# Earlier conditions, a reordered gate and shorter seams in a fused mixture-of-experts, attention and feed-forward kernel

## The chip, the cores and the metric

The kernel runs on one core of a Trainium2 chip. The metric is the device time of one execution in microseconds (us), lower is better. In the text PE is TensorE (matrix engine), DVE is VectorE, ACT is ScalarE, POOL is GpSimd and SP is SyncE, which here only issues transfers. "PEld" is the loading of weights into PE.

## The reference

Everything is float32. The input x has 4 sequences of 512 tokens with 256 features; there is also one condition vector of 64 values per sequence.

```
x   = x + linear_attention(mixture_of_experts(x, condition))
out = x + two_local_layers(condition_attention(x, condition))

mixture_of_experts: gate = rmsnorm(x) @ wg + wg_b + condition @ gg_W + gg_b       # 8 experts
                    the two largest of softmax(gate), each times
                    relu(relu(x W1 + b1) W2 + b2) W3 + b3 of its expert
linear_attention:   blocks of 32 tokens, 8 heads, features elu(q proj) + 1, elu(k proj) + 1
                    out = num * 1 / (qp . sum(kp) + 1e-8), then @ w_out.T + b_out
condition_attention: 16 heads over 512 tokens, the weights scaled by
                    sigmoid(tanh([x, condition] Wc1 + bc1) Wc2 + bc2), renormalised;
                    0.79 of that plus 0.21 of a field weight fa:
                    fp = layernorm(relu(condition We1 + be1) We2 + be2),
                    fa = softmax(fp @ sin-table.T)
two_local_layers:   token shift, local attention with window 128, GEGLU feed-forward, twice
```

What the change calls "the conditions" is the part that needs the condition vector alone: condition @ Wc1 (`csb`), the vector `fp`, and the field weights `fa`, transposed to `faT`. They depend on no token, and are used only in the condition attention.

## The kernel before

**Stages.** One program goes through the stages in time: gate and routing (0 to 40 us of the span), expert slots (40 to 321), a conditional block for two rare slots and the weighted sum of the experts' results (321 to 337), linear attention (337 to 500), condition attention (500 to 745), the two local layers (745 to 1427). A scheduler orders each engine's instructions. Inside a region `with PE.in_order()` PE's order is the order in which the code is written; generators are advanced by `next` to weave two pieces of work into each other.

**Gate.** The tokens are loaded into `xres[0..3]`, each 128 partitions x 1024. PE first multiplies the condition with the gate's weights (`pgb`), then transposes the tokens (`pxt`, 32 transposes). The copies `xT` from the accumulators alternate between ACT and DVE (`evac`). ACT squares a batch at once (line 1167), DVE sums it (`ss`, line 1168). PE computes the logits (`pg`); a Sqrt and a reciprocal give `rstd`; `pgt` transposes the logits back and DVE forms `gate` (lines 1192 and 1195). A long DVE chain then picks the two experts and gives every chosen token a row (`rowtok`, line 1342).

**Expert slots.** 20 slots always run, two more (`NRARE`) run under `tc.If`. A slot has 128 or 256 token rows of one expert. `loads` brings that expert's weights with three SP transfers whose address depends on the routing. `gather` fetches the token rows with POOL's indirect transfers and transposes them (`pxb`, `xbT`). `layer` makes h1 and h2 (`ph`, then a relu on ACT or DVE in turn), and `last` makes `po`, adds the bias and scatters the rows to `ys` in DRAM. The first gather is covered by filler matmuls, `busy(4)`; `busy(n)` is n products of the identity with `xres[0]`, whose results nobody reads. They appear as `pbusy`.

**Loads and conditions.** The table `later` holds 15 loads of weights of the next stages (among them `rows`, the 795 KB of row constants `crows`), one is issued per slot from slot 2 on. `conditions` runs ahead of the last of the 20 slots: `pcs` (condition times weights), `pfp`, a DVE and ACT chain to `fp` (lines 241 to 251), `pfpT` (its transpose), `pfs` (512 field logits), an Exp to `fa` (line 263), `pfaT`.

**Seam of the conditional block.** After it come `busy(13)` and four batches of: two loads `g` of 512 KB each (line 1477, from `ys`), four ACT products (line 1481), four DVE sums to `ymoe` (line 1482).

**Linear attention.** `front(b)` adds the constant row `bo` to `xres[b]` on POOL (line 1496), transposes `ymoe` to `yT` and makes `qk` (`pqk`) and `v`. `features` gives `pf` and `f`, `scores` gives `sc`, `values` gives `pn`, `pz`, the reciprocal `z` (line 1565) and `aT` (line 1566), `tail` gives `pao` and adds it into `xres[b]` (line 1576). The accumulators of the features come from the pool `fe`. After the last `tail`, the condition attention begins with its own `front(0)`: transposes `pt` of `xres[0]`, `xT2`, then `pcq`, `pck`, `pcv` and the coherence products `pct`, before the first attention scores (`sc`, `cex`).

Of the kernel before, what the change touches and what calls it, by code (L numbers as in the profile page):

```python
# [63 lines left out]
def adaln_attn_ffn_kernel(ctx: ExitStack, tc: tile.TileContext, a: dict, out: bass.AP):  # L64
# [141 lines left out]
    def cond_weights(pool, queued=lambda name, load: load()):  # L206
        loads = {
            "rows": lambda: load_rows("crows", pool),
            "wqkv": lambda: weight("cwqkv", [128, 2, 3 * H], chunks(a["c_wqkvT"]), pool),
            "hmask": lambda: weight("hmask", [128, 10], a["hmask"], pool),  # L210
            "wout": lambda: weight("cwout", [128, 2, H], chunks(a["c_woT"]), pool),
# [16 lines left out]
    def conditions(W, cp):  # L228
# [22 lines left out]
        nc.vector.tensor_tensor(fp, fp, row("lnb")[:B, :], ALU.add)  # L251
        pt = tpt("pfpT")
# [12 lines left out]
        nc.vector.tensor_scalar(fa, fa, fsum, FIELD, ALU.mult, ALU.mult)  # L265
        pt = tpt("pfaT")
# [6 lines left out]
    def cond_stage(W, cp, sp, safe):  # L273
        csb, faT = W["csb"], W["faT"]
        y = [resp.tile([128, NT, H], F32, tag="res", name=f"yc{b}") for b in range(B)]
        if not safe:

            v1s = []
            for i in range(2):
                v1 = cp.tile([128, NT, CH, 32], F32, tag=f"v1{i}", name=f"v1{i}", bufs=1)  # L280
                nc.gpsimd.memset(v1, 0.0)
                nc.gpsimd.memset(v1[:, :, :, CHD : CHD + 1], 1.0)
                v1s.append(v1)

        def front(b, d):
            xT2 = cp.tile([128, 2, S], F32, tag="xT2", name="xT2")
            xs = cp.tile([128, 2], F32, tag="xs", name="xs")
            for c in range(2):
# [3 lines left out]
                nc.vector.tensor_copy(xT2[:, c, :], pt)  # L292
# [8 lines left out]
            kT = cp.tile([128, 2, S], F32, tag="kT", name="kT")  # L301
            for c in range(2):
# [6 lines left out]
                yield  # L309
                ps = mmt("pck")  # L310
                mm(ps, [(W["wqkv"][:, k, H + c * 128 : H + (c + 1) * 128], xT2[:, k, :]) for k in range(2)])
                nc.vector.tensor_scalar(kT[:, c, :], ps, col("bk", c), None, ALU.add)
# [211 lines left out]
        run(front(0, ds[0]))  # L524
# [23 lines left out]
    def local_stream(dw, lp, y, dr):  # L548
# [264 lines left out]
        ds = [SimpleNamespace(ps={}, oT={}) for b in range(B)]  # L813
        with PE.in_order():
            run(front(wa, 0, ds[0]))
# [292 lines left out]
    with ExitStack() as abc:  # L1108
# [7 lines left out]
        with ExitStack() as moe:  # L1116
# [27 lines left out]

            wgs = xp.tile([128, 2, 32], F32, tag="wgs", name="wgs")
# [6 lines left out]
            with PE.in_order():  # L1152
                pgb = acct("pgb")
                for b in range(B):
                    PE.matmul(pgb[:, b * NE : (b + 1) * NE], csB[:, b, :], ggw, start=True, stop=True)
                xTs = []
                for b in range(B):
                    if b % 2 == 0:
                        xT = ew.tile([128, 4, ME], F32, tag="w2", name="xT")
                    for c in range(2):  # L1160
# [3 lines left out]
                        evac(xT[:, b % 2 * 2 + c, :], pt)  # L1164
# [276 lines left out]
            for j, d in enumerate(often):  # L1441
                if j == len(often) - 1:
                    conditions(cw_, wp)
# [42 lines left out]
        with ExitStack() as lin:  # L1486
# [65 lines left out]
            def values(d, g):  # L1552
                if g == 0:
                    d.aT = lp.tile([128, 2, S], F32, tag="aT", name="aT")
# [217 lines left out]
```

## Time and profile before

| what | value |
|---|---|
| median of three runs | 1429.75 us (1427.66 to 1430.11) |
| the profiled execution's own time | 1429.31 us |
| its span | 1427.5 us (1.8 us of the time lie around it) |
| instructions | 19422 |
| mean granted TensorE clock | 0.981 |
| PE busy 0 to 40 / 40 to 321 / 321 to 337 | 19.6 of 40.0 / 275.1 of 281.0 / 12.9 of 16.0 us |
| PE busy 337 to 500 / 500 to 745 / 745 to 1427 | 143.9 of 163.0 / 236.7 of 245.0 / 666.0 of 682.0 us |
| granted clock in those stages | 0.79, 1.00, 0.89, 0.94, 0.99, 0.99 |

How to read the views: a row of the timeline has the start, the busy time, the engine, the line, the operation, its output and inputs, the shape, and how many instructions it joins; in brackets stands the idle time before it on its engine and what ended it. Most matmuls have the line of one helper (L78 a product, L82 a transpose), so they are told apart by the name of their output. One float32 product has two records. In the table of waits the columns are the total, how often, and the longest. The granted clock is the share of full speed that PE was given; at 0.5 a matmul takes twice as long.

### The profile page before, as it was taken

Reading aid. Unit: us, or ns where it says so; the run is one execution under the profiler, and the core shown is the slowest. Engines: PE = TensorE matmul, PEld = TensorE weight load, DVE = VectorE, ACT = ScalarE, POOL = GpSimd, SP = SyncE. Lnnn points to the kernel's source line nnn. Section 1 sums busy time; section 2 is a strip of 40 time slices with the busy share of each in tenths; the row PEclk is TensorE's granted clock in tenths of the full one; section 3 lists DMA queues with packets and bytes.
Section 4 is the critical chain, followed back from the end, with each engine's and each line's share of the span. In section 5 each row is a group of like instructions: output and inputs, shape, how many; then the busy total and the mean of one; then the engine's idle time right before and its main releaser. Section 6 shows DMA issues by size and latency. Waiting matters only on the chain.

```text
span 1427.5 us, 19422 instructions
## 1 busy us (share of the span) xinstructions
PE 1354.0 (95%) x7624; PEld 835.6 (59%) x7624; DVE 667.0 (47%) x1297; ACT 586.0 (41%) x969; POOL 230.4 (16%) x219
## 2 busy tenths in 40 slices
PE   4999999998899799999999999999999999999998
PEld 3788888874566543333335555656655456556564
DVE  6222221223677642333226777754352767854331
ACT  3111111123555325554654647563222567474111
POOL 0324232111000020000102322100020312310010
PEclk8999999999999899999999999999999999999999
DMA  3577667623000000000111011211001010011000
GB/s 122 216 258 264 223 227 247 214 79 122 1 2 1 0 1 0 1 1 1 44 49 64 2 36 35 75 33 30 22 0 41 23 32 23 17 39 47 14 23 25
DMA packets 43645, 94.74 MB, mean 66 GB/s; under 512 B 9760, under 2 KB 25752, under 8 KB 40728
## 3 DMA queue, kind: packets, MB, share of 16 engines
q1 hardware_dynamic: 38984, 83.11, 17.6%
q0 software_dynamic: 3552, 9.70, 2.0%
q8 instruction: 63, 1.03, 0.3%
q10 hardware_dynamic: 1008, 0.58, 0.2%
q14 instruction: 38, 0.31, 0.1%
HBM read 84.08 MB, written 7.21 MB: 64 GB/s over the span
## 4 chain that ended last, share of the span: by engine, by line
PE 66%; DVE 5%; ACT 3%; issue 2%; DMA 1%; SPq 0%; DVEq 0%; POOL 0%; POOLq 0%
PE pdq L78 11%; PE pug L78 5%; PE sc L78 5%; PE pua L78 5%; PE pv L78 5%; PE pn L78 4%; PE pfy L78 4%; PE pdy L78 4%; PE pds L78 4%; PE pz L78 2%; PE pqt L82 2%; PE pqk L78 2%; PE pcq L78 1%; PE pur L78 1%; PE pcv L78 1%
## 5 line engine op out<-in xcount | busy, mean ns | idle before, releaser
L78 PE MATMUL pdq<-wqkv,yT 128*128 128x512 f32 x384 | 177.6, 603 | 4.5 <-ACT yT L583 4.5
L403 ACT ACTIVATE cex<-sc 128x1024 f32<-128x1024 f32 x128 | 124.1, 1021 | 95.8 <-PE sc L78 94.7
L78 PE MATMUL ph<-h,w 128*128 128x256 f32 (+1 forms) x704 | 133.4, 347 | 1.0 <-ACT h L1356 0.5
L653 DVE TENSOR_TENSOR p<-p,lmask 128x384 f32<-128x384 f32 (+1 forms) x128 | 98.4, 786 | 66.5 <-ACT p L651 65.0
L609 POOL TENSOR_TENSOR qr<-t,t 128x512 f32<-128x512 f32 x64 | 85.8, 1340 | 247.5 <-DVE t L606 229.8
L78 PEld LDWEIGHTS ph<-h,w 128*128 128x128 f32 x704 | 116.2, 191 | 13.3 <-DVE h L1358 0.7
L78 PEld LDWEIGHTS pdq<-wqkv,yT 128*128 128x128 f32 x384 | 69.5, 190 | 82.2 <-issue 72.8
L1358 DVE TENSOR_SCALAR h<-ph,w 128x256 f32<-128x256 f32 (+1 forms) x88 | 36.1, 438 | 164.5 <-PE ph L78 101.5
L1356 ACT ACTIVATE h<-ph,w 128x256 f32<-128x256 f32 (+1 forms) x88 | 35.4, 438 | 187.1 <-PE ph L78 132.5
L651 ACT ACTIVATE p<-pds,ss 128x256 f32<-128x256 f32 (+1 forms) x256 | 95.6, 457 | 35.8 <-PE pds L78 27.3
L78 PE MATMUL pug<-hT,w 128*128 128x512 f32 x160 | 78.3, 612 | 0.0
L599 ACT ACTIVATE sq<-pdq 128x512 f32<-128x512 f32 x64 | 38.3, 598 | 96.7 <-PE pdq L78 57.6
L78 PE MATMUL sc<-qm,kT 32*128 32x512 f32 x512 | 76.0, 647 | 0.0
L78 PE MATMUL pua<-hT,w 128*128 128x512 f32 x160 | 75.6, 595 | 0.0
L78 PE MATMUL pv<-cex,v 128*32 128x512 f32 x512 | 69.0, 604 | 1.7 <-DVE xT L292 1.7
L78 PE MATMUL ph<-xbT,w 128*128 128x256 f32 (+1 forms) x352 | 68.3, 346 | 0.0
L78 PE MATMUL po<-w,h 128*128 128x256 f32 x296 | 67.7, 380 | 0.5 <-ACT h L1356 0.5
L78 PE MATMUL pdy<-wo,oT 128*128 128x256 f32 x256 | 63.3, 392 | 3.3 <-DVE oT L693 3.3
L78 PE MATMUL pds<-qT,kT 64*128 64x256 f32 (+1 forms) x512 | 65.3, 375 | 0.0
L78 PEld LDWEIGHTS pds<-qT,kT 64*128 64x128 f32 x512 | 43.9, 186 | 32.9 <-issue 26.2
L78 PEld LDWEIGHTS ph<-xbT,w 128*128 128x128 f32 x352 | 58.4, 191 | 6.9 <-issue 0.9
L78 PE MATMUL pfy<-w,uA 128*128 128x256 f32 x256 | 61.2, 382 | 0.0
(294 smaller groups left out, 2103.5 us busy)
## 6 DMA issues: line engine op xcount, KB each, us to landing
w<-in_moe_w_dram SPq DMA_DIRECT2D x22, 1024.0 KB
w<-in_moe_w_dram SPq DMA_DIRECT2D x22, 640.0 KB
w<-in_moe_w_dram SPq DMA_DIRECT2D x22, 516.0 KB
zb<-rows SPq DMA_DIRECT2D x32, 256.0 KB
g<-ys SPq DMA_DIRECT2D x8, 512.0 KB
wqkv<-in_f_wqkv_dram SPq DMA_DIRECT2D x2, 1536.0 KB
w<-in_f_w_dram SPq DMA_DIRECT2D x2, 1408.0 KB
xres<-in_x_dram SPq DMA_DIRECT2D x4, 512.0 KB
```

The costliest lines, as they stand in the source:

```text
L78: cls._queue(nc.tensor.matmul(*args, **kw))
L82: cls._queue(nc.tensor.transpose(*args, **kw))
L403: nc.scalar.activation(ex, pss[j], AF.Exp, scale=CHD**-0.5)
L599: nc.scalar.activation(sq, p3, AF.Square)
L609: nc.gpsimd.tensor_tensor(qr_t[:, s], t1, t2, ALU.add)
L651: nc.scalar.activation(p[:, at], pss[r][:, at], AF.Exp, scale=d.ss[:, 2 * u + jj, 1, 2 * c + r : 2 * c + r + 1])
L653: nc.vector.tensor_tensor(p[:, :n], p[:, :n], lmask[:, :n], ALU.mult)
L1356: nc.scalar.activation(dst, src, AF.Relu, bias=bias)
L1358: nc.vector.tensor_scalar(dst, src, bias, 0.0, ALU.add, ALU.max)
```

## The change

- Gate: `pgb` comes after the transposes; all eight `xT` copies go to DVE; each batch is squared by four ACT instructions that also sum (`accum_out`), and the DVE sums go away. The reciprocal of `rstd` keeps its place in the program order.
- Conditions: their weights and `rows` are loaded right behind the tokens. `conditions` becomes a generator with three pieces: the first ahead of `busy(4)`, the second after the products of slot 0, the third after those of slot 1. The table `later` shrinks to nine loads.
- The instruction order after the change also puts the POOL additions of `bo` for batches 1 to 3 ahead of the first gather; they need only the tokens and `rows` and the readers of the tokens to be done.
- Seam of the conditional block: `busy(3)` stands before it and `busy(6)` after it. `results(b)` issues the loads of batch b, in halves for batch 0; those of batches 2 and 3 are issued in `front(0)` and `front(1)`. `weighted(0)` stays at the seam, `weighted(1..3)` move into `front(b)`.
- Seam to the condition attention: the last `tail` is handed to `cond_stage` and woven into `front(0)`, in which `pck` now precedes `pcq`; for batch 0 ACT makes `xT2` and `kT`. The last batch's `aT` and `awo` move to the pool `wp`, the last reciprocal and product are split in halves, the two PSUM pools of the stage change places, and the tiles `v1` are set later.
- Seam to the local layers: the first `front` is taken out of the pinned region.

```diff
@@ cond_weights / conditions
+            "wout": lambda: weight("cwout", [128, 2, H], chunks(a["c_woT"]), pool),
             "wqkv": lambda: weight("cwqkv", [128, 2, 3 * H], chunks(a["c_wqkvT"]), pool),
             "hmask": lambda: weight("hmask", [128, 10], a["hmask"], pool),
-            "wout": lambda: weight("cwout", [128, 2, H], chunks(a["c_woT"]), pool),
...
         nc.vector.tensor_tensor(fp, fp, row("lnb")[:B, :], ALU.add)
+        yield
         pt = tpt("pfpT")
...
         nc.vector.tensor_scalar(fa, fa, fsum, FIELD, ALU.mult, ALU.mult)
+        yield
         pt = tpt("pfaT")
@@ cond_stage
-    def cond_stage(W, cp, sp, safe):
+    def cond_stage(W, cp, sp, safe, before=()):
...
-                nc.vector.tensor_copy(xT2[:, c, :], pt)
+                (nc.scalar.copy if b == 0 else nc.vector.tensor_copy)(xT2[:, c, :], pt)
...
+            if not safe and b < 2:
+                make_v1()
+            for c in range(2):
+                ps = mmt("pck")
+                mm(ps, [(W["wqkv"][:, k, H + c * 128 : H + (c + 1) * 128], xT2[:, k, :]) for k in range(2)])
+                if b == 0:
+                    nc.scalar.activation(kT[:, c, :], ps, AF.Identity, bias=col("bk", c))
+                else:
+                    nc.vector.tensor_scalar(kT[:, c, :], ps, col("bk", c), None, ALU.add)
+                yield
...
-                ps = mmt("pck")
-                mm(ps, [(W["wqkv"][:, k, H + c * 128 : H + (c + 1) * 128], xT2[:, k, :]) for k in range(2)])
-                nc.vector.tensor_scalar(kT[:, c, :], ps, col("bk", c), None, ALU.add)
-                yield
...
-        run(front(0, ds[0]))
+        first = front(0, ds[0])
+        with PE.in_order():
+            for _ in range(4):
+                next(first)
+            for _ in before:
+                next(first)
+        run(first)
@@ local layers
+        run(front(wa, 0, ds[0]))
         with PE.in_order():
-            run(front(wa, 0, ds[0]))
@@ gate
+            cw_ = {}
+            soon = ("rows", "wc1c", "we1", "we2", "peT", "csT")
+            loads_ = cond_weights(wp, lambda name, load: load)
+            for name in soon:
+                cw_[name] = loads_.pop(name)()
...
-                pgb = acct("pgb")
-                for b in range(B):
-                    PE.matmul(pgb[:, b * NE : (b + 1) * NE], csB[:, b, :], ggw, start=True, stop=True)
...
-                        evac(xT[:, b % 2 * 2 + c, :], pt)
+                        nc.vector.tensor_copy(xT[:, b % 2 * 2 + c, :], pt)
...
-                    nc.scalar.activation(sq, xres[b], AF.Square)
-                    nc.vector.reduce_sum(ss[:, b * NT : (b + 1) * NT], sq, axis=AX.X)
+                    for t in range(NT):
+                        nc.scalar.activation(sq[:, t, :], xres[b][:, t, :], AF.Square,
+                                             accum_out=ss[:, b * NT + t : b * NT + t + 1])
+                pgb = acct("pgb")
+                for b in range(B):
+                    PE.matmul(pgb[:, b * NE : (b + 1) * NE], csB[:, b, :], ggw, start=True, stop=True)
...
-            nc.vector.reciprocal(rstd, rstd)
+            tc.keep_in_program_order(nc.vector.reciprocal(rstd, rstd))
@@ expert slots
+            aside = conditions(cw_, wp)
+            next(aside)
             busy(4)
...
-                "awo": lambda: weight("awo", [128, 2, H], chunks(a["a_woT"]), wl),
+                "awo": lambda: weight("awo", [128, 2, H], chunks(a["a_woT"]), wp),
...
+                **loads_,
             }
-            cond_weights(wp, lambda name, load: later.update({name: load}))
...
-                if j == len(often) - 1:
-                    conditions(cw_, wp)
...
                 d.h2 = layer(d, h1, "h2", d.w2, 4)
+                next(aside, None)
             last(len(often) - 1, often[-1])
+
+            busy(3)
             with tc.If(halves > NHALF - NRARE):
...
-            busy(13)
-            for b in range(B):
-                gs = []
-                for k in range(2):
-                    g = gp.tile([128, NT, H], F32, tag=f"g{k}", name=f"g{k}", bufs=2)
-                    at = 1 + (k * B + b) * S
-                    nc.sync.dma_start(g, ys[at : at + S].rearrange("(t p) h -> p t h", p=128))
-                    gs.append(g)
+            busy(6)
+            def results(b):
+                gs = [gp.tile([128, NT, H], F32, tag=f"g{k}", name=f"g{k}", bufs=2) for k in range(2)]
+                n = 2 if b == 0 else NT
+                for t in range(0, NT, n):
+                    for k in range(2):
+                        at = 1 + (k * B + b) * S + t * 128
+                        nc.sync.dma_start(gs[k][:, t : t + n, :],
+                                          ys[at : at + n * 128].rearrange("(t p) h -> p t h", p=128))
+                return gs
+
+            def weighted(b, gs):
                 for t in range(NT):
                     i = b * NT + t
                     nc.scalar.mul(gs[0][:, t, :], gs[0][:, t, :], tops[0][:, i : i + 1])
                     nc.vector.scalar_tensor_tensor(
                         y[b][:, t, :], gs[1][:, t, :], tops[1][:, i : i + 1], gs[0][:, t, :], ALU.mult, ALU.add)
+            both = {b: results(b) for b in range(2)}
+            weighted(0, both[0])
@@ linear attention
             def front(b, d):
+                if b:
+                    weighted(b, both[b])
+                if b + 2 < B:
+                    both[b + 2] = results(b + 2)
...
-                    d.aT = lp.tile([128, 2, S], F32, tag="aT", name="aT")
+                    pool, tag = (wp, "aTlast") if d is ds[-1] else (lp, "aT")
+                    d.aT = pool.tile([128, 2, S], F32, tag=tag, name="aT")
...
-                nc.vector.reciprocal(z, z)
-                nc.vector.tensor_tensor(d.aT[:, g, :], pn, z, ALU.mult)
+                n = S // 2 if d is ds[-1] and g == 1 else S
+                for at in range(0, S, n):
+                    half = slice(at, at + n)
+                    nc.vector.reciprocal(z[:, half], z[:, half])
+                    nc.vector.tensor_tensor(d.aT[:, g, half], pn[:, half], z[:, half], ALU.mult)
...
-            run(tail(B - 1, ds[B - 1]))
+            end = tail(B - 1, ds[B - 1])
...
+            sp = cst.enter_context(tc.tile_pool(name="sp", bufs=3, space=PSUM, reuse_waits="tile"))
             cst.enter_context(banks("ps1", mm=2))
-            sp = cst.enter_context(tc.tile_pool(name="sp", bufs=3, space=PSUM, reuse_waits="tile"))
...
-            y = cond_stage(cw_, cp, sp, False)
+            y = cond_stage(cw_, cp, sp, False, end)
```

More of the change, by code (lines that the diff above doesn't have):

```diff
@@ L271, in conditions, with make_v1 @@
         W["csb"], W["faT"] = csb, faT
-    def cond_stage(W, cp, sp, safe):
+    def cond_stage(W, cp, sp, safe, before=()):
         csb, faT = W["csb"], W["faT"]
         y = [resp.tile([128, NT, H], F32, tag="res", name=f"yc{b}") for b in range(B)]
[L276 to L283, printed above, removed]
+        v1s = []
+        def make_v1():
+            i = len(v1s)
+            v1 = cp.tile([128, NT, CH, 32], F32, tag=f"v1{i}", name=f"v1{i}", bufs=1)
+            nc.gpsimd.memset(v1, 0.0)
+            nc.gpsimd.memset(v1[:, :, :, CHD : CHD + 1], 1.0)
+            v1s.append(v1)
         def front(b, d):
@@ L1429, in adaln_attn_ffn_kernel @@
                 "aqkv": lambda: weight("awqkv", [128, 2, 3 * H], chunks(a["a_wqkvT"]), wl),
-                "awo": lambda: weight("awo", [128, 2, H], chunks(a["a_woT"]), wl),
+                "awo": lambda: weight("awo", [128, 2, H], chunks(a["a_woT"]), wp),
                 "aproj": lambda: weight("aproj", [128, 2, 2, NF], a["a_proj"], wl),
                 "bmask": lambda: weight("bmask", [128, 4, 128], a["bmask"], wl),
+                **loads_,
             }
-            cond_weights(wp, lambda name, load: later.update({name: load}))
-            cw_ = {}
             ds = [SimpleNamespace() for _ in SLOTS]
@@ L1642, in adaln_attn_ffn_kernel @@
                 W = cond_weights(wp)
-                conditions(W, wp)
+                run(conditions(W, wp))
                 y = cond_stage(W, cp, None, True)
```

## The prediction

> **What bounds the kernel now.** I read the page first, then TensorE's waits, then the windows and the timeline at the places the change touches. All times in us unless said.
>
> ```profile
> PE 1354.0 (95%) x7624; PEld 835.6 (59%) x7624; DVE 667.0 (47%) x1297; ACT 586.0 (41%) x969; POOL 230.4 (16%) x219
> ```
>
> TensorE (PE) is busy 95% of the 1427.5 span and is 66% of the chain that ended last. Anything that does not close a PE hole, shorten PE work in PE's own order, or end a half-clock stretch is worth nothing. The waits that PE has at the seams in question:
>
> ```profile
> PE pgb L78 <- DVE csB L1150: 7.8, 1, 7.8
> ...
> PE pao L78 <- DVE aT L1566: 5.0, 2, 3.9
> ...
> PE pbusy L78 <- issue: 3.4, 1, 3.4
> PE pqk L78 <- DVE yT L125: 3.3, 3, 2.1
> ...
> PE pfpT L82 <- DVE fp L251: 1.5, 1, 1.5
> ```
>
> The columns are total, times, longest. In the timeline the conditions cost PE time in the last slots (own work plus a wait for `fp`), and the If seam is thirteen filler passes and what follows:
>
> ```profile
> 308.79 0.28 PE L82 MATMUL pfpT<-ident,fp 4*128 4x4 f32 x2 [1.46 <-DVE fp L251]
> 309.33 1.88 PE L78 MATMUL pfs<-peT,fpT 128*4 128x512 f32 x4 [0.26 <-DVE fpT L256]
> ```
> ```profile
> 324.11 13.09 PE L78 MATMUL pbusy<-xres,ident 128*128 128x512 f32 x26 [3.38 <-issue]
> 324.44 10.76 SPq L1477 DMA_DIRECT2D g<-ys  x8
> ...
> 329.79 1.67 DVE L1482 SCALAR_TENSOR_TENSOR ymoe<-g,m,g 128x256 f32<-128x256 f32 x4 [8.59 <-DMA g<-ys]
> ...
> 337.04 1.04 PE L82 MATMUL pt<-ident,ymoe 128*128 128x128 f32 x8
> ...
> 337.16 3.77 DVE L1482 SCALAR_TENSOR_TENSOR ymoe<-g,m,g 128x256 f32<-128x256 f32 x4 [2.91 <-ACT g L1481]
> 337.29 2.57 POOL L1496 TENSOR_TENSOR xres<-xres,crows 128x1024 f32<-128x1024 f32 x1 [13.20 <-PE pbusy L78]
> ...
> 340.85 0.68 DVE L125 COPY yT<-pt 128x512 f32<-128x512 f32 x1
> ...
> 341.58 4.54 PE L78 MATMUL pqk<-yT,awqkv 128*128 128x512 f32 x6 [2.10 <-DVE yT L125]
> ```
>
> Three things: the first batch's sum is ready at 331.5, but its transposes sit behind the filler until 337.04; then four DVE sums take 3.77 where the same four took 1.67, while POOL adds `bo`; and `yT` queues behind them. The last seam is the wait for the reciprocal and its slow aftermath:
>
> ```profile
> 490.19 3.35 DVE L1565 RECIPROCAL z<-z 128x512 f32<-128x512 f32 x1 [2.75 <-ACT z L1564]
> ...
> 494.40 5.31 PE L78 MATMUL pao<-awo,aT 128*128 128x256 f32 x12 [3.90 <-DVE aT L1566]
> ```
>
> [...] after the hole of 490 to 494 the granted clock is 0.50 from 494 to 498. [...]
>
> **The change, part by part** (minus is a gain; starts and durations are of the profiled execution, 1429.31, whose span is 1427.5; the median is 1429.75, 0.44 above it. 0.2%, about 2.9, is what a measurement can tell from no change).
>
> 1. *Gate.* PE does its 32 transposes before the four `pgb` pairs; DVE takes all eight `xT` copies (0.64 each); four ACT squares (1.06) and four DVE reductions (1.2) become 16 ACT squares that sum themselves. Price: 0.43 for a 128x256 ACT (1.71/4 at L1481) plus 0.18 for the accumulator read at L263: 16 x 0.61 = 9.8 from 5.53 gives 15.3; table load 1.28, `rstd` 0.31, reciprocal 0.25: 17.1. PE's branch: the eight copies end near 12.8, `pgb` 1, `pg` 2.2, `gT` 0.69, `pgt` 0.66: 16.6. The gate product, now at 19.47, could start near 17.1: -2.4. Against it: `crows` now lands behind the tokens, so POOL's adds of `bo` for batches 1 to 3 (6.98 for three at 131 now) need no longer wait for the slots. By the instruction order they stand before the first gather, for xres landed (10.6) plus crows (some 2.3 more): about 13.3 to 20.3. The gate chain after the product is DVE instructions with two SBUF inputs, and would stand still till 20.3. I take **+0.4**; ends -2.5 (no lock) and +1.5.
>
> 2. *Conditions, first two pieces.* Piece one (`pcs`, `pfp`, 2.3 of PE) goes before the four filler passes in the first gather's hole, PE idle but for filler (39.6 to 44.17): free; if the hole were full, 2.3. On DVE `csb` goes between the two `rowtok` instructions (40.08), so the gather is 0.37 late: +0.4. The `fp` chain with its table load ends near 46.6, beside the gather. Slot 0: the second tile's transposes go before the first `ph` (+0.4), `pfpT` 0.28 and `pfs` 1.88 stand on PE's path, `pfaT` 0.41 after slot 1; with small relu stalls **+3.0** (2 to 4.5). The ACT table loads (two of 1.28) lie ahead of `xbT` evacuations; that is the top end. SP's six extra loads go behind xres, ahead of the expert weights; those wait for the routing at 40, so nothing queues behind them (zero; cover: 27 of idle SP queue).
>
> 3. *Last slots.* From 301.42 to the last `po` at 320.73 is 19.3. Without the conditions: `ph` 2.05, `po` 3.72, `ph` 3.75, a relu wait 0.5, `po` 2.0: 12.0 to 12.3. **-7.0** (6 to 7.5): `pcs`+`pfp` 2.3, wait for `fp` 1.46, `pfpT`+`pfs` 2.35, `pfaT` 0.41, relu wait 0.5.
>
> 4. *If seam.* 13 filler passes become 3 before the branch and 6 after; the first batch's `g` is loaded in halves, batches 2 and 3 when their fronts start; `weighted(1..3)` moves into the linear attention. PE resumes 3.38 after its last work; the branch on each engine stays. In before's clock: `g` is issued 3.7 after the last `po`, as now (324.44); half-size transfers land about 0.7 sooner than the 3.9 of now; first batch's sum by 331 instead of 331.5; filler ends 5 to 6.5 after the branch at half clock, about 330; transposes 1.05, `yT` 0.7, `pqk` 3.45, first `pf` at 337.8 instead of 346.05. The `bo` adds of batches 1 to 3 are gone from here, that of batch 0 still waits for the filler, and meets fewer sums. **-8.0** (-6 to -10.5: the lower end is a filler wholly at half clock and the lock on `yT`).
>
> 5. *Linear attention.* Twelve DVE sums (0.42) and twelve ACT products (0.43) come beside features and scores, 1.7 a batch, between `qk`, `f` and `ex` on their engines. PE is busy 17 to 19.7 of each 20 here, DVE and ACT have slack; **+0.8** (0 to +5, three times 1.7 in full). On SP the late `g` loads wait for buffers with nothing behind them till 707.
>
> 6. *Seam to cond.* The last `tail` is handed to the cond front; PE goes `pz`, `pt` of batch 0, four `pck`, `pao`, `pcq`. Eight `pt` (1.05) and `pck` (3.4, as two full-clock `pqk`) cover the 3.9 hole; `pao` then runs at full clock (12 passes at 0.21 instead of 5.31: -2.7). Hole 3.9 + half clock 2.7 + pieces of 0.88 and 0.63 afterwards = 8.1; `pao` second half may still wait for `aT`. **-7.4** (-5 to -8.5). Halved reciprocals are issued recip, recip, aT, aT, hence nothing for them.
>
> 7. *Local seam.* Taking the local front out of the pinned region leaves every engine's order the same: 0, both ways.
>
> Sum: 0.4 + 3.0 - 7.0 - 8.0 + 0.8 - 7.4 = **-18.2**; 1429.3 - 18.2 = **1411**.
>
> **The rivals.**
> *Lock does not bite* (POOL's adds done before the chain, or DVE first): for it, crows might land early; against, the 2.1 lost at 337. Then -2.5 instead of +0.4: 1408. Chance 0.25.
> *Given back*: `weighted(1..3)` and the late `g` stall PE in the linear attention (+5 instead of +0.8), and the six filler passes run at half clock with the lock on `yT` (-6): 1411 + 4.2 + 2 = 1417. For it: fronts already wait for `f` (4.7 over four waits); against, the slack. Chance 0.2.
> *Slower, cold clock*: the filler is there to hold the clock; with nine passes instead of 13, split by the branch, the clock could stay at 0.5 well into the linear attention. Each us at half clock loses 0.5, so 18 are cancelled only by 36 at half clock. Near 1429.5 at that point, 1433 beyond. The longest half-clock stretch inside busy work is about 7 (342 to 346, 492.6 to 499.4), and the ones of 16 (22 to 38) have PE mostly idle. Chance 0.04.
> *Parts not done*: piece 7 has this answer already; were 4 also without effect, 1419. Chance 0.06.
>
> **How the numbers follow.** Mine 0.45 at 1411, its own range 1407 to 1415. The best ends together give 1402, the worst 1423; 8 in 10 lie between 1402 and 1420. Faster 0.94 (all but the cold clock and a mishap of like size), same 0.03, slower 0.03.
>
> **What would show it.** Step 1: gate product near 17 or 20, POOL's L1532 at 13 to 20, long DVE entries beside it. Step 2: `pcs` near 40, first `ph` near 47, `pfs` in slot 0. Step 3: no `pcs` at 301; 12 from there to the last `po`. Step 4: three `pbusy` before the If, first `pf` 8 earlier. Step 5: PE's busy share between first `pf` and last `pz`. Step 6: no PE hole over 1 between `pz` and `pct`, clock 1.0 there. The forecast is wrong if the clock in the linear attention falls below 0.9, if the span from first `ph` to the last slot grows by over 6, or the stages after 520, whose work and order are the same, change by over 2.

## The result, and the profile after

The changed kernel took 1416.85 us (median of five runs, 1414.33 to 1421.13) against 1429.75 (five runs, 1427.66 to 1432.64): the ratio is 0.9914, 95% interval 0.9889 to 0.9938, some 12 us faster. In a second series of executions it took 1414.65 (six runs) against 1427.79 (eleven runs), ratio 0.9917 (0.9901 to 0.9933). The forecast was 1411 within 1402 to 1420: right in direction and inside its range, but the gain is 12 to 13 where 18 were forecast, and the first median lies a little outside the 1407 to 1415 that the forecast gave its own case.

The profiled execution took 1414.33, the lowest of its five; its span is 1412.6, 14.9 below the span before. Its page, the line of busy times:

```profile
span 1412.6 us, 19454 instructions
...
PE 1347.5 (95%) x7616; PEld 832.5 (59%) x7616; DVE 662.8 (47%) x1295; ACT 588.0 (42%) x997; POOL 229.7 (16%) x219
```

PE still is the bound. It is busy 6.5 less: four filler passes fewer (0.86 each at full clock, 3.4); the rest, less work at half clock among it, was not told apart. TensorE's waits after the change (total, times, longest):

```profile
PE pxt L82 <- DMA xres<-in_x_dram: 7.3, 3, 5.0
...
PE pt L82 <- DVE ymoe L1511: 2.8, 1, 2.8
...
PE ph L78 <- DVE h L1385: 2.1, 1, 2.1
...
PE pao L78 <- DVE aT L1608: 1.1, 1, 1.1
...
PE pbusy L78 <- PEq L1486: 0.3, 1, 0.3
```

The waits of 7.8 for `pgb`, 3.9 for the last `aT`, 3.4 at the branch and 1.5 for `fp` are gone. New are the wait for the tokens (PE now has nothing else to do then), 2.8 for the first batch's sums, and 2.1 for a relu in the first slot.

The stages, by the same instruction in each trace, with a second trace of the changed kernel (from the second series). All in us; the columns are differences to the trace before. A stretch ends where the next begins; `po` is the last product of an expert slot, `sc` the first scores of the condition attention.

| stretch | forecast | trace 1 | trace 2 |
|---|---|---|---|
| start to `ptot` (gate, pick) | +0.4 | +1.70 | +2.17 |
| `ptot` to the end of the first slots, `pfaT` with them | +3.0 | +5.45 | +2.15 |
| last slots, to the end of the last `po` | -7.0 | -7.83 | -7.82 |
| from there to the first `pf` | -8.0 | -7.16 | -5.74 |
| first `pf` to last `pz` (linear attention) | +0.8 | +1.52 | +0.29 |
| last `pz` to the first `sc` | -7.4 | -8.17 | -7.46 |
| first `sc` to the end | 0 | -0.41 | +0.45 |
| sum | -18.2 | -14.9 | -16.0 |

Both traces are of the fastest execution of their series (1414.33 and 1413.27), so their sums lie 2 to 3 above the 12.9 and 13.1 between the medians. That part of the miss lies in executions without a trace, and no stage can be named for it.

The head of the changed kernel in its timeline:

```profile
5.01 3.46 PE L82 MATMUL pxt<-ident,xres 128*128 128x128 f32 x16 [5.01 <-DMA xres<-in_x_dram]
...
11.86 1.94 PE L82 MATMUL pxt<-ident,xres 128*128 128x128 f32 x8 [0.78 <-DMA xres<-in_x_dram]
...
13.73 1.88 PE L78 MATMUL pgb<-ggw,csB 64*128 64x8 f32 x8
...
14.59 6.96 POOL L1532 TENSOR_TENSOR xres<-xres,crows 128x1024 f32<-128x1024 f32 x3 [13.11 <-DMA cwe<-in_c_we2T_dram]
...
15.53 3.31 PE L78 MATMUL pg<-xT,wgs 128*32 128x512 f32 x16
...
20.42 0.29 DVE L1217 TENSOR_TENSOR gate<-pgt,rstd 128x128 f32<-128x128 f32 x1 [0.59 <-PE pgt L82]
20.74 0.95 DVE L1220 TENSOR_TENSOR gate<-gate,gb 128x128 f32<-128x128 f32 x1
```

PE starts 2.8 earlier than before, but runs dry while the third and fourth batch land (1.54 and 0.78 idle); `pgb` then stands ahead of `pg`, and `pg` takes 3.31 (before 2.21), with a granted clock of 0.50 from 11.56 to 18.39. The gate product at 20.42 is later than before (19.47), and the next DVE instruction, which has two SBUF inputs, takes 0.95 instead of 0.29 and ends at 21.69: it waits for POOL, whose three additions end at 21.55. This wait is what the forecast and the expectations call the lock.

The seam of the conditional block:

```profile
319.89 2.74 PE L78 MATMUL pbusy<-xres,ident 128*128 128x512 f32 x6
...
322.19 0.97 POOL L1450 DMA_INDIRECT ys<-ob,goal  x1 [2.96 <-DMA ys<-ob,goal]
322.93 5.39 PE L78 MATMUL pbusy<-xres,ident 128*128 128x512 f32 x12 [0.30 <-PEq L1486]
...
325.17 11.65 SPq L1503 DMA_DIRECT2D g<-ys  x10
...
328.41 2.33 POOL L1532 TENSOR_TENSOR xres<-xres,crows 128x1024 f32<-128x1024 f32 x1 [3.54 <-PE pbusy L78]
328.71 3.50 DVE L1511 SCALAR_TENSOR_TENSOR ymoe<-g,m,g 128x256 f32<-128x256 f32 x4 [8.19 <-DMA g<-ys]
...
331.08 2.43 PE L82 MATMUL pt<-ident,ymoe 128*128 128x128 f32 x8 [2.76 <-DVE ymoe L1511]
...
333.39 4.89 PE L78 MATMUL pqk<-yT,awqkv 128*128 128x512 f32 x8
...
338.21 1.98 PE L78 MATMUL pf<-qk,aproj 32*128 32x512 f32 x8
```

Filler no longer holds the transposes; the sums do (3.50 instead of 1.67, beside POOL's addition to `xres[0]`), and ahead of them the last scatter, which waited for an earlier scatter, so that `g` is issued 5.12 after the last `po` and not 3.71 as before. `pt` and `pqk` run partly at half clock (0.50 from 332.41 to 335.83): `pqk` takes 4.89.

The seam to the condition attention has no hole:

```profile
483.04 1.09 PE L82 MATMUL pt<-ident,xres 128*128 128x128 f32 x8
484.37 3.70 PE L78 MATMUL pck<-xT,cwqkv 128*128 128x512 f32 x8 [0.24 <-ACT xT L296]
487.91 1.89 PE L78 MATMUL pao<-awo,aT 128*128 128x256 f32 x8
```

### The profile page after: what moved, and what is told of

The parts are those of the page before. It is cut to its first block, busy times and chain, and to the rows that moved or that the text cites. A ratio compares the mean times of both kernels' runs of the same rounds, so it can differ in the third digit from the quotient of the medians.

```text
span 1412.6 us, 19454 instructions
## 1 busy us (share of the span) xinstructions
PE 1347.5 (95%) x7616; PEld 832.5 (59%) x7616; DVE 662.8 (47%) x1295; ACT 588.0 (42%) x997; POOL 229.7 (16%) x219
## 3 DMA queue, kind: packets, MB, share of 16 engines
q1 hardware_dynamic: 39016, 83.11, 18.2%
## 4 chain that ended last, share of the span: by engine, by line
PE 86%; DVE 6%; ACT 3%; DMA 2%; issue 2%; another core or an unknown queue 0%; SPq 0%; POOLq 0%; DVEq 0%; POOL 0%
PE ph L78 13%; PE pdq L78 12%; PE pug L78 5%; PE pua L78 5%; PE sc L78 5%; PE pv L78 5%; PE pfy L78 5%; PE po L78 4%; PE pn L78 4%; PE pdy L78 4%; PE pds L78 4%; PE pz L78 2%; PE pqt L82 2%; PE pqk L78 2%; PE pck L78 1%
## 5 line engine op out<-in xcount | busy, mean ns | idle before, releaser
L78 PEld LDWEIGHTS ph<-h,w 128*128 128x128 f32 x704 | 115.8, 191 | 14.9 <-DVE h L1385 2.3
L667 ACT ACTIVATE p<-pds,ss 128x256 f32<-128x256 f32 (+1 forms) x256 | 95.4, 456 | 36.2 <-PE pds L78 27.7
```

What stands on the lines that cost most here:

```text
L78: cls._queue(nc.tensor.matmul(*args, **kw))
L667: nc.scalar.activation(p[:, at], pss[r][:, at], AF.Exp, scale=d.ss[:, 2 * u + jj, 1, 2 * c + r : 2 * c + r + 1])
```

## The experiments

The first eight variants were executed once each, and took 1412.07 to 1419.71 as a whole (the kernel before, beside them, 1427.40 and 1421.17). Whole times of single executions of one kernel differ by 5 us and more, so these are read by stage, each stretch from its own starting instruction.

### The gate: PE's order or POOL's additions

First edit, `pgb` back in front:

```diff
             with PE.in_order():
+                pgb = acct("pgb")
+                for b in range(B):
+                    PE.matmul(pgb[:, b * NE : (b + 1) * NE], csB[:, b, :], ggw, start=True, stop=True)
                 xTs = []
```

> The changed kernel with the four gate products of the condition (pgb) again ahead of the 32 token transposes, all else as changed. In the changed kernel the gate product starts at 20.42 us, the pick of the experts ends at 25.4 and the first row list (rowtok, second instruction) is at 41.83. Theory A (PE's own order sets the head: pgb stands between the transposes and pg for 1.9, and pg runs at half clock, 3.3 instead of 2.2, because PE idles between the token arrivals): the gate product moves to 18.0 to 19.0, pg is at full clock; the row list comes 0.7 to 2 earlier, less what the lock then costs. Theory B (POOL's three additions of bo, 14.6 to 21.5[...]): the gate product may move, but the chain stays blocked to 21.5 and the row list stays within 0.3 of 41.8.

Second edit, `bo` in a tile of its own that is loaded late:

```diff
             later = {
+                "bo": lambda: weight("bo2", [128, H], a["crows"][bo_at : bo_at + bo_n].partition_broadcast(128), wp),
...
-                    xres[b], xres[b], row("bo").unsqueeze(1).to_broadcast([128, NT, H]), ALU.add)
+                    xres[b], xres[b], cw_["bo"].unsqueeze(1).to_broadcast([128, NT, H]), ALU.add)
```

> The changed kernel with the row bo in a tile of its own that is loaded in the third slot, so that POOL adds it to batches 1 to 3 there and not beside the gate. Theory B (lock): the gate chain no longer meets POOL; if the lock were what ate the gain of the gate, the gate product and all behind it come 2 us or more earlier (row list at 39.8 or before). Theory A (PE's order): the gate product stays at 20.4 within 0.2, only the second gate instruction shrinks from 0.95 to 0.29, the row list comes 0.5 to 0.8 earlier (41.0 to 41.3).

Both:

> Both edits at once: pgb ahead of the transposes and the row bo loaded in the third slot. Theory A with the lock as a second, hidden limit: the gate product at 18.0 to 19.0 and nothing blocked behind it, the row list at 39.2 to 40.2, that is 1.6 to 2.6 before the changed kernel, more than the two single edits together if the lock hides the first one's gain. Rival (the ACT squares with table load, done at 15.2 in the changed kernel, set the start): the same as the sum of the single edits.

The heads of eight traces (three of these kernels are described further below). "rows early" means that POOL's additions stand beside the gate. Four more traces, of variants that do not touch the gate, have the changed kernel's head, with `ptot` at 26.08 to 26.84; so the new gate took 1.0 to 2.7 longer than the old one in all seven traces that have it.

| kernel | `pgb` | `bo` | `pg` took | gate product at | from it to `ptot` | `ptot` at |
|---|---|---|---|---|---|---|
| before | first | late | 2.21 | 19.47 | 4.64 | 24.11 |
| changed, trace 1 | after | rows early | 3.31 | 20.42 | 5.39 | 25.81 |
| changed, trace 2 | after | rows early | 1.92 | 19.40 | 6.88 | 26.28 |
| fillers read rows | after | rows early | 1.92 | 17.74 | 7.41 | 25.15 |
| `pgb` first | first | rows early | 2.58 | 18.78 | 6.78 | 25.56 |
| `bo` late | after | late | 1.92 | 18.75 | 4.72 | 23.47 |
| `bo` own tile | after | late | 3.64 | 22.50 | 4.73 | 27.23 |
| both | first | late | 2.49 | 18.80 | 4.73 | 23.53 |

Two limits, and each can hide the other. With the rows early the chain's end does not follow the gate product: where the product starts at 17.74 to 19.40, `ptot` comes 3.61 after POOL's last addition in each of these traces (for trace 2, 15.66 + 7.01 = 22.67, and 26.28). With `bo` late it is 4.7 behind the product. The lines of the first edit and of both, gate product and its successor:

```profile
18.78 0.29 DVE L1217 TENSOR_TENSOR gate<-pgt,rstd 128x128 f32<-128x128 f32 x1 [0.59 <-PE pgt L82]
19.11 0.65 DVE L1220 TENSOR_TENSOR gate<-gate,gb 128x128 f32<-128x128 f32 x1
...
25.56 0.56 PE L78 MATMUL ptot<-ones,pick 128*128 128x1 f32 x2 [6.82 <-DVE pick L1260]
```
```profile
18.80 0.29 DVE L1217 TENSOR_TENSOR gate<-pgt,rstd 128x128 f32<-128x128 f32 x1 [0.59 <-PE pgt L82]
19.13 0.29 DVE L1220 TENSOR_TENSOR gate<-gate,gb 128x128 f32<-128x128 f32 x1
...
23.53 0.56 PE L78 MATMUL ptot<-ones,pick 128*128 128x1 f32 x2 [4.76 <-DVE pick L1260]
```

The gate product is the same, the pick comes 2.03 sooner: that is POOL's price, and the first edit alone gave only 0.25. Of the first two expectations neither theory was quite right. With `pgb` first the product moved as theory A said (18.78), and the row list hardly, to 41.56, as theory B said. `bo` late moved the row list to 39.90, near the 39.8 of the lock theory, but the product itself had moved by 1.67, since `pg` ran at full clock in that execution. DVE does not stand still for all three additions: in these traces an instruction with two SBUF inputs that starts beside an addition ends just behind it. In the kernel whose fillers read the rows, the additions run from 14.53 to 21.54, some 2.34 each:

```profile
18.07 1.27 DVE L1220 TENSOR_TENSOR gate<-gate,gb 128x128 f32<-128x128 f32 x1
19.37 0.29 DVE L1236 TENSOR_REDUCE m<-gate 128x16 f32<-128x128 f32 x1
19.70 1.99 DVE L1237 TENSOR_TENSOR eqs<-gate,m 128x128 f32<-128x128 f32 x1
```

L1220 ends at 19.34, just behind the second addition (some 19.2); the reduction, with one input, takes 0.29 beside the third; L1237 ends at 21.69, just behind the third. With the first edit the same two take 0.65 and 1.99 and end at 19.76 and 22.10, the second and third addition at some 19.62 and 21.96. The gate product, with one of its inputs from PSUM, takes 0.29 beside an addition too (at 17.74 and 18.78). The second limit is PE's order. With `pgb` behind the transposes the product lay anywhere from 17.7 to 22.5, depending on when the tokens came and on the clock that the products met (`pg` took 1.92 to 3.64). PE idles between the token transfers there (1.54 and 0.78 in trace 1, 3.02 in trace 2), and some of its work behind that is slow: in both traces eight transposes take 1.94 that take 1.07 elsewhere in trace 1. That the idle time brings the half clock is an inference. With `pgb` first the product lay within 18.7 to 19.2 in four traces. Even with both limits lifted the new gate is worth only 0.2 to 0.7 (`ptot` at 23.46, 23.53 and 23.88 in three traces, against 24.11), not the 2.4 that its ACT branch alone would allow.

### The first gather's hole without filler

```diff
-            busy(4)
+            busy(0)
```

> The changed kernel without the four filler passes in the first gather's hole (pieces of the conditions stay). In the changed kernel the pieces and the filler run at half clock from 42 to 46 and end at 48.4; the first gathered rows are transposed at 48.33, while 3.6 after their issue at 42.29 would be 45.9. Theory A (the filler has become the bound, since it now starts 4.3 later behind the pieces): the transposes start at 45.8 to 46.3 and the first ph 1.5 to 2.5 earlier than 49.17, unless the clock falls. Theory B (the gather is what is late, by its place behind the other transfers): first transposes stay at 48 or later. Theory C (the clock): without filler the first slot runs at half clock, ph of 2.0 becomes 3 to 4 and the gain is gone.

The transposes came 4.1 after the row list (46.24 against 42.11) where the changed kernel's trace 1 has 6.5: the filler had been the bound there (theory A). But:

```profile
46.24 1.10 PE L82 MATMUL pxb<-ident,xb 128*128 128x128 f32 x3 [1.87 <-DMA xb<-in_x_dram,rowtok]
...
49.03 3.60 PE L78 MATMUL ph<-xbT,w 128*128 128x128 f32 x16
```

The first layer takes 3.60 at half clock (0.50 from 44 to 52) instead of 1.95 (theory C), and from the row list to the second slot's products it is 22.2 against 20.2 in the nine traces with the filler at full clock. By this one trace the four passes earn their place, some 2.0. In those nine the transposes start 4.9 after the row list, so in trace 1 it was the half clock (0.50 from 42.28 to 45.69) that made the pieces and the filler outlast the gather; no other trace with these fillers had it except the one with the last tail ahead. The wait of 2.1 for a relu in trace 1 stood in none of the other traces with this order of the first slot; its cause stays open.

### The filler after the block reads other data

`busy` gets a second argument, the tile that it multiplies:

```diff
-            busy(6)
+            busy(6, cw_["rows"])
```

> The changed kernel, but the six filler passes after the conditional block multiply the row constants instead of xres[0], so that POOL's addition of bo to xres[0] waits only for the three passes ahead of the block. In the changed kernel that addition ran from 328.4 to 330.7 and the four DVE sums of batch 0 took 3.50 instead of 1.67, PE waiting 2.8 for them. Theory[...]: the addition moves to 323 to 326, the sums take 1.7, the transposes of the first batch come 1.5 to 2.0 earlier after the last po (9.0 to 9.6 instead of 11.0), the first pf likewise. Rival (the transfers of g set the sums, the lock only fills a wait): the transposes stay 10.7 to 11.3 after the last po.

```profile
320.06 2.35 POOL L1533 TENSOR_TENSOR xres<-xres,crows 128x1024 f32<-128x1024 f32 x1
...
325.52 0.88 DVE L1512 SCALAR_TENSOR_TENSOR ymoe<-g,m,g 128x256 f32<-128x256 f32 x2 [8.39 <-DMA g<-ys]
326.06 0.72 PE L82 MATMUL pt<-ident,ymoe 128*128 128x128 f32 x2 [1.08 <-DVE ymoe L1512]
...
328.62 0.88 DVE L1512 SCALAR_TENSOR_TENSOR ymoe<-g,m,g 128x256 f32<-128x256 f32 x2 [2.21 <-ACT g L1511]
329.16 1.16 PE L82 MATMUL pt<-ident,ymoe 128*128 128x128 f32 x6 [2.37 <-DVE ymoe L1512]
...
330.61 5.24 PE L78 MATMUL pqk<-yT,awqkv 128*128 128x512 f32 x8 [0.29 <-ACT yT L123]
```

The lock is gone, and the first transposes start 9.4 after the last `po` instead of 11.0, as the theory said. The first `pf` is not earlier (19.1 after the last `po`, against 18.2 and 19.6 in the changed kernel's two traces): the second half of `g` comes 2.9 behind the first and now holds the rest, and behind PE's pause of 2.4 `pqk` takes 5.24, where the next one takes 3.70. The two traces of the three edits together, described below, have these fillers as well; the one that issued `g` as early as trace 1 has its transposes at 9.3 and its first `pf` at 18.4. The five traces without the edit that issued `g` then have theirs at 11.0 to 11.1 and at 17.9 to 19.6. So the rival decides the stage: the transfers set it, the lock only filled a wait.

### The conditions back in the last slots

```diff
-            aside = conditions(cw_, wp)
-            next(aside)
...
+                if j == len(often) - 1:
+                    run(conditions(cw_, wp))
...
-                next(aside, None)
```

> The changed kernel with all of the conditions back ahead of the last of the 20 slots; their weights and the rows are still loaded behind the tokens. Theory A: the last slots grow by 7.0 to 7.8 (from the last ph<-xbT to the last po and what stands before it), the first slots shrink by 2 to 3 against an undisturbed first slot (13.6 from first ph to the second slot's h products becomes 11.8 to 12.1) plus 0.3 to 0.4 for csb between the row-list instructions and 0.35 for pfaT: net 4 to 5 slower than the changed kernel. Rival (the wait of 2.1 for h and the half-clock filler of the changed kernel's trace belong to the early conditions): the first part shrinks by 5 or more and the move nets 2 or less.

From the second slot's products to the end of the last `po` it takes 261.9 instead of 254.8: 7.2 more (`pfaT` is in both). From `ptot` to these products it takes 34.8 against 36.2 to 36.7 in the traces without disturbance, so 1.4 to 1.9 less, with one slow spell (49 to 52, the first layer 3.22 instead of 1.95) among them. By these two stretches the move of the conditions is worth about 5, near theory A. One thing came with it that was in no forecast: `g` is issued 3.72 after the last `po`, as before the change, where it was 5.1 to 7.2 in all traces with the conditions early.

```profile
324.36 0.97 POOL L1448 DMA_INDIRECT ys<-ob,goal  x1 [9.14 <-DVE ob L1443]
```

Here the last scatter waits for its own data. In the changed kernel the last slots are so short that it waits for an earlier scatter's end. So `g` is issued 1.4 or more later, and part of the 7.8 gained in the last slots is given back at the seam: the first `pf` comes 17.7 after the last `po` here, and 18.2 and 19.6 after it in the changed kernel's traces. From `ptot` to the first `pf` the move is left with 2.1 (trace 1, with its disturbed first slot) or 4.0 (trace 2).

The wait itself comes in two sizes. In seven of the twelve traces with the conditions early `g` is issued 5.1 to 5.4 after the last `po`, in five 7.1 to 7.2, as the chain of scatters happens to land; none of the edits touches the scatters, and why they land as they do stays open. The first `pf` follows: 17.9 to 19.6 with the early issue, 20.4 to 21.9 with the late one (without the thirteen fillers, below). So about 2 us between these traces come from here.

### The last tail ahead of the condition front

```diff
-            end = tail(B - 1, ds[B - 1])
+            run(tail(B - 1, ds[B - 1]))
+            end = ()
```

> The changed kernel, but the last tail of the linear attention is finished before the condition attention's front begins (its tiles, pools and the order of pck and pcq as changed). Theory A (the weave fills the wait for the reciprocal and so keeps the clock): from the last pz to the first sc 28 to 31 instead of 23.0, with a hole of 3.5 to 4 and a granted clock of 0.5 behind it. Rival (other parts of that seam bring the gain: pck first, ACT's copies, the pools): 23 to 25.

From the last `pz` to the first `sc` 28.2 instead of 23.0. The hole and the cold stretch are back:

```profile
483.15 4.54 PE L78 MATMUL pao<-awo,aT 128*128 128x256 f32 x12 [3.39 <-DVE aT L1608]
```
```profile
484.00:486.00 2.00, 2.00 (x6) 1.60 (x5) 0.57 (x1) 0.00 (x0) 0.00 (x0) 0.50 0.04 8
```

(The second fence is a row of the windows: stretch, its length, busy time of PE, PEld, DVE, ACT and POOL, then the granted clock.) So the weave is worth 5.2 of the 8.2. The other 2.9 was not told apart: it may lie in the rest of that seam's edits, or in the clock, since the trace before has 6.83 at half clock behind that hole and this one 3.41.

### Thirteen fillers after the block

```diff
-            busy(6)
+            busy(13)
```

> The changed kernel with thirteen filler passes after the conditional block instead of six (three ahead of it stay). Theory A (first sums are what PE waits for in the changed kernel, so part of the longer filler is free): the filler ends 6 later (334), the transposes come 13.5 to 14.5 after the last po instead of 11.0, the first pf 2.5 to 3.5 later. Rival (cold clock: the short filler lets the clock fall in the linear attention): the transposes come later, but the linear attention from first pf to last pz takes 142 instead of 144.9, giving back 2 or more.

The transposes came 14.1 after the last `po`, as theory A said. But the first `pf` came 8.5 later than in trace 1 (26.6 after the last `po`), because the scheduler put the products of batches 1 and 2 ahead of `yT` on ACT, and these wait for their transfers; 2.1 of the 8.5 goes with a later issue of `g` (7.2 after the last `po`), and the earlier scatter that this issue hangs on was already late before the filler began. The linear attention took 140.5 instead of 144.9, more than the rival had asked for. But the sums of all later batches were now done ahead of it, so its gain is in part work moved out of the stage; the last section reads the clock's part. From the last `po` to the last `pz` together it is 167.2, against 163.1 and 163.3 in the changed kernel's traces.

### The edits together

> The changed kernel itself, on the chip and in the rounds of the three variants that follow, so that they can be compared with it. Median within 0.3% of 1416.85, and the stages that no edit touches the same; single executions spread by 5 us or more if the spells at half clock fall differently in each.

> The changed kernel with the row bo in a tile of its own, loaded in the third slot, in the pool that is closed ahead of the condition attention (in the earlier form of this edit the tile stood in the pool that stays open and the weights of the local layers came 45 us later). [...] the row list comes near 39.9 and the median is 1.5 to 2.5 below the changed kernel; the local layers' weights are issued near 690 again and nothing is lost at 735. If the gain at the head is eaten by the clock's spells, the row list is early and the medians are equal within 1.

Against the second edit above only the pool differs:

```diff
-                "bo": lambda: weight("bo2", [128, H], ... , wp),
+                "bo": lambda: weight("bo2", [128, H], ... , wl),
```

> Three edits together on the changed kernel: bo in its own tile (as in the run before this one), pgb ahead of the transposes, and the six fillers after the conditional block reading the row constants. By the single runs: 2.2 at the row list, 1.0 at the first rows' transposes where the filler ran at half clock, 0 to 1.6 at the block's seam: 3 to 4 below the changed kernel, near 1413. Rival: the spells of half clock that the single runs showed after the seam eat it, and it is within 1.5 of the changed kernel.

> As the run before, with seven fillers instead of six after the block. If the clock falls because PE stands idle for 2.4 between the halves of the first batch, one more pass (0.9) does not change it: pqk stays at 5.2 and the total within 1 of the run before. If it is the gap ahead of the first half that counts, pqk runs at full clock (3.6) and the first pf comes 1.5 earlier.

| kernel | median (runs) | ratio to before | 95% interval |
|---|---|---|---|
| changed | 1414.65 (6) | 0.9917 | 0.9901 to 0.9933 |
| `bo` own tile | 1415.46 (6) | 0.9909 | 0.9888 to 0.9930 |
| three edits | 1411.42 (4) | 0.9894 | 0.9876 to 0.9911 |
| three edits, seven fillers | 1413.37 (5) | 0.9907 | 0.9891 to 0.9922 |

`bo` in its own tile alone brought nothing that shows: in its profiled execution the gate product lay at 22.50, behind a `pg` at half clock (3.64), so in that execution the removed lock had nothing to free. The three edits together have the lowest median, 3.2 below the changed kernel, but the intervals overlap, and a version with one more filler pass lies 1.3 below; a gain of 1 to 3 is likely, not secured. Whether a seventh filler shortens `pqk` is not shown. `pqk` took 5.81 with seven and 5.08 with six, but the two traces differ ahead of it: with seven, the last scatter waited longer and `g` was issued 7.15 after the last `po`, against 5.19 with six:

```profile
319.41 0.97 POOL L1451 DMA_INDIRECT ys<-ob,goal  x1 [3.82 <-DMA ys<-ob,goal]
...
322.38 12.18 SPq L1506 DMA_DIRECT2D g<-ys  x10
```

The tile's place mattered too. In the earlier form, in the pool that stays open, PE waited for the local layers' weights:

```profile
737.49 4.78 PE L78 MATMUL pdq<-wqkv,yT 128*128 128x512 f32 x6 [5.24 <-DMA wqkv<-in_f_wqkv_dram]
```

That load was issued at 730.8, with the tile in the other pool at 695.5. Why is inferred: 1 KB a partition moved it onto memory that is freed later. From the first `sc` to the end those two kernels took 916.6 and 916.8, the one with the other pool 907.4, and this is why they were not faster as a whole (spans 1415.4 and 1414.7).

## Why the prediction was right, and what was mis-sized

**Head (step 1), +0.4 forecast, +1.7 and +2.2 measured.** The effect was right in kind: POOL's additions moved ahead of the gather, and DVE's two-input instructions waited for them (0.95 for 0.29 in trace 1; 0.74 and 1.99 for 0.29 in trace 2), each for the addition then running. That the whole chain would stand still until the last addition's end was the author's estimate. Three terms were mis-sized. The end of the additions was put at 20.3; it was 21.5 to 22.7, since they start at 14.5 to 15.7 and not at 13.3. PE's branch to the gate product was put at 16.6; it ended at 17.7 to 22.5. Its own terms add up to 17.35 (12.8 + 1 + 2.2 + 0.69 + 0.66), and it left out that PE runs dry between token transfers and that `pgb` and `pg` may run at half clock (1.88 and 3.31 in trace 1, 1.05 and 1.92 in trace 2). ACT's branch was put at 17.1, with 0.61 for each of 16 squares; they came 0.40 apart, and `rstd` ended at 15.19 before its reciprocal, so ACT was not what the gate waited for; the table load ahead of `rstd` took the 1.28 that it had before. The rival that the lock does not bite fell: without it `ptot` is 2.0 earlier.

**First slots (step 2), +3.0; +2.2 where nothing disturbed it.** "Free in the hole" held in most traces and failed in trace 1, where the pieces and filler ran at half clock and outlasted the gather by about 1. Another 2.1 of trace 1 is the unexplained wait. The additions (`csb` 0.33, `pfpT` and `pfs` about 2, `pfaT` 0.4) were as priced.

**Last slots (step 3), -7.0; -7.8 in both traces.** The remaining work was put at 12.0 to 12.3; it is 11.5.

**Seam of the block (step 4), -8.0; -7.2 and -5.7.** The sum assumed that `g` is issued 3.7 after the last `po`, "as now". It was 5.1 or more, since the shorter last slots made the last scatter wait for an earlier one. Half-size transfers were put 0.7 sooner than 3.9, an estimate; ACT's first product of `g` began 2.74 after the issue (before 3.88). The sum took the lock on the sums of the experts' results as its lower end; it did occur (3.50 instead of 1.67), but the second half of the transfers would have held PE as long (2.9 behind the first half where the lock was gone). Half clock at `pqk` (4.89 to 5.86 instead of 3.45) adds 1.4 to 2.4. Against these stood a reserve that the forecast did not name: its own terms from the first sum at 331 (1.05 + 0.7 + 3.45) end at 336.2, and it put the first `pf` at 337.8.

**Linear attention (step 5), +0.8; +1.5 and +0.3.** The difference of the two traces is one spell of half clock; at equal spells it is +0.3, so the moved sums lie in slack, and the rival "given back" does not hold for them. That rival had put the whole at 1417, and the first median is 1416.85; this is a coincidence, since its main term, +5 in this stage, did not come, and only its -6 at the seam of the block was near.

**Seam to cond (step 6), -7.4; -8.2 and -7.5.** As priced, with the halved reciprocals without effect, as forecast: DVE still does both, then both products.

**Local seam (step 7), 0; -0.41 and +0.45.** The order was the same and so was the time.

That the total fell into the range is in part luck. Four steps lie outside their own ends in one trace or both (the head above +1.5, the first slots of trace 1 above +4.5, the last slots beyond -7.5, the seam of the block in trace 2 short of -6), and these misses cancel in part. The head and the seam of the block fell short by 0.8 to 2.3 each, the last slots and the seam to cond gave 0.1 to 0.8 more.

The slower case, a clock that stays cold deep into the linear attention, did not come: three or four spells of 3.4 each in that stage, as before the change (three), where 36 of half clock would have been needed to undo the gain.

## What to carry to other kernels

A step that is made faster needs every one of its branches costed, and the engine that a freed load lets start early belongs to the sum: here an early load of row constants let POOL start additions beside the gate, and the gate gained nothing while they stood there; once they were away, what was left hung on PE's order and clock. When a stage before a transfer gets shorter, look at what queues ahead of that transfer (the last scatter here). Filler passes are priced by what runs behind them: four in the first hole were worth 2, seven more after the block cost more than came back behind them (4 in all, of which 2 go with the late issue of `g`).

## What the runs showed of the hardware

**The clock fell in spells of 3.41 us on a fixed grid.** In every trace the stretches with a granted clock of 0.5 (the records begin 7.7 to 21.0 into the span) last 3.41 or a multiple of it (but for one cut off by the end of the program), and their starts lie a multiple of 3.41 apart. Before the change those from 320 to 500 start at 325.32, 342.38, 362.86, 468.68 and 492.57, that is 5, 6, 31 and 7 times 3.41 apart; the first three last 3.41, the other two 6.83. The stretch ahead of a spell need not be idle: the clock fell at 492.57, only 2.1 into the hole that the prediction reads, and in the 3.41 ahead of that PE was busy for 1.33. What makes it fall was not shown. In the kernel without filler the first layer took 3.60 in a spell instead of 1.95. What was not expected is how well one number then orders the traces. The linear attention, from the first `pf` to the last `pz`, by the spells in it:

| spells | time of the stage (traces) |
|---|---|
| 1 | 140.5 (thirteen fillers) |
| 2 | 141.7 to 142.2 (seven traces) |
| 3 | 143.6 to 143.7 (four traces, the changed kernel's trace 2 among them); before the change 143.4 |
| 4 | 144.9 (changed kernel, trace 1) |

From row to row a spell goes with 1.2 to 1.9, and the edits hardly show. (In the first row work had moved out of the stage, as said above.) The changed kernel's two traces differ here by one spell with the same instructions in the same order; the windows show it as 0.89 and 0.96 (trace 1) against 0.79 and 0.99 (trace 2):

```profile
344.00:360.00 16.00, 14.05 (x71) 9.31 (x70) 10.23 (x14) 11.18 (x15) 0.00 (x0) 0.89 0.00 1
360.00:483.00 123.00, 112.42 (x1003) 76.42 (x1001) 86.95 (x87) 62.98 (x69) 1.80 (x1) 0.96 0.01 1
```
```profile
344.00:360.00 16.00, 14.05 (x64) 8.20 (x63) 8.76 (x13) 9.78 (x12) 0.00 (x0) 0.79 0.00 1
360.00:483.00 123.00, 111.95 (x1015) 76.42 (x1014) 88.78 (x89) 64.57 (x72) 3.88 (x4) 0.99 0.00 1
```

So part of a difference between two single executions of this kernel goes with the number of their spells, and another part, it seems, with how the last scatters land: a gain of 1 or 2 us at one place can be undone by one spell more at another, and only stage times, or many runs, tell.
